# The start of the expert stage: the first chunk's features on another DMA queue, and all bias matrices made at the beginning

## The chip, the cores and the metric

The kernel runs on one core of a Trainium2 chip. The metric is the device time of one execution in microseconds (us); lower is better. Engines: TensorE (PE) does matrix products, VectorE (DVE), ScalarE (ACT) and GpSimd (POOL) do elementwise work, and SyncE (SP) issues most of the DMAs. GpSimd issues DMAs too, on a second queue that is fed by software. Everything is in float32.

## What is computed

Two images of 256 channels and 64x64 positions (4096 tokens each) go through three blocks: a selective-scan block, a bidirectional selective-scan block, and a dense mixture of eight experts. The change concerns the mixture alone, which in the reference is

```
feat = mean over the batch of x                    # x: layer-normed tokens [batch, token, 256]
w    = softmax(feat @ Wr + br)                     # per token, 8 experts; shared by both images
h    = relu(bn(x @ W1[e] + b1)); h = relu(bn(h @ W2[e] + b2))
y    = h @ Wo[e] + bo[e]
out  = t + sum over e of y * w[:, e]
```

## The kernel before

The work is in two stages. The long first stage runs both scan blocks, with DVE and POOL nearly always busy. It also fills TensorE's spare time: as soon as 512 tokens of one image are final, their features are normed and written to DRAM (`nf_dram`), and some of their expert outputs are computed early and written to DRAM (`u_dram`).

The second stage, here called the last stage, does what is left. Work is cut into chunks of 512 tokens, `i` = 0 to 7, for each image `b`. `first[b, i]` is the number of experts that were done early for that chunk. In this build the list of chunks that are not finished, `rest`, is 4, 3, 2, 1, 5, 0. In five of them image 1 has all eight experts left (`first` is 0), and in chunk 5 it has two left (`first` is 6); image 0 is finished everywhere. That makes 42 pairs of a chunk and an expert, taken one after another.

For each pair TensorE runs two layers from PSUM to SBUF through ScalarE (`layer`, matmuls on L1326, evictions on L1330). VectorE then multiplies the result by the token's expert weight (`weigh`, L1337), and three pairs later TensorE runs the third layer and adds into a PSUM tile `y` (`last_layer`, L1350). Before a chunk's first pair in `last_layer`, `y` is opened with a product of the expert weights `wts` and the output biases (L1344). The biases are a matrix `bo_k` of 8 rows by 256, of which the rows below `k = first[b, i]` are zero. `late_bias` makes it: for `k` = 0 a DMA, for another `k` a memset on VectorE (L1305) and then a DMA by SyncE (L1306). It makes each once, at the first call. The kernel before calls it once at the beginning, for chunk 4 (`bo_0`), and otherwise from within `last_layer`, when a chunk is opened. So `bo_6` is made when chunk 5 is opened.

The router's weights come from the sum of both images' features (`both`, for chunk 4 an addition on POOL, L1211), the product with `wr` (`logits`, L1228), a softmax in small steps on VectorE and ScalarE, a transpose (`spread`, L1253), and a trip through DRAM to spread them over partitions (L1257 out, L1259 back). `wr` is scaled on VectorE once (L1379), after its DMA.

Each engine and each queue runs its instructions in the order in which the program emits them. Weights `W1`, `W2`, `Wo` of an expert are loaded by SyncE (`load_w`, L1319) and stay in SBUF. In each round of the loop three matrices are loaded (four in the first), until all are there. Early outputs (`u`, L1274) and residuals (`x`, L1270) are loaded by SyncE too, and added on VectorE (L1275, L1276). The features of chunk 4, for both images, are loaded by POOL's queue (`load_n`, L1182), as are `wr` and `br` (L1377, L1378). In that queue they stand behind the stores of the first stage's last early outputs (L1024).

The beginning of the last stage in the kernel before:

```
load_n(chunks[0])                                   # POOL's queue: chunk 4, both images
wr = ...; br = ...                                  # POOL's queue
nc.vector.tensor_scalar(wr, wr, 1.0 / NB, ...)      # L1379
for name, e in [W1, W2 of expert 0; W1, W2 of 1]:   # SyncE
    load_w(name, e)
late_bias(first[NB - 1, rest[0]])                   # bo_0: SyncE
layer_norm(rest[0]); both(rest[0])                  # no work here; POOL adds
...
for at, (b, i, e) in enumerate(pairs):              # loads, then two layers, ...
```

Of the kernel before, what the change touches and what calls it, by code (L numbers as in the profile page):

```python
# [48 lines left out]
NB, C, L = 2, 256, 4096  # L49
# [33 lines left out]
E = 8  # L83
# [53 lines left out]
def hybrid_kernel(ctx: ExitStack, tc: tile.TileContext, a: dict, out: bass.AP):  # L137
    nc = tc.nc
# [55 lines left out]
    with ExitStack() as st:  # L194
# [790 lines left out]
        def emit_experts(put):  # L985
# [40 lines left out]
            for b, c, e, times in put:  # L1026
                key = {"tag": f"{b}{c}_{e}"}
                early[b, c] = e + 1
                if e == 0:
                    at = max(before.get(0, 0) + 3, min(r[0] for r in ready if r[1:] == (b, c)))  # L1030
                    sl.put(at, "sp", lambda b=b, c=c: load_n(b, c))
                sl.put(times[0], "pe2", lambda b=b, c=c, key=key: key.update(n=n[b, c]))
                for l, (x, dst) in enumerate((("n", "h1"), ("h1", "h2"), ("h2", "u"))):
                    at = before.get(l, times[0] - 6) + 3
                    sl.put(at, "sp", lambda l=l, e=e, key=key: load_w(l, e, key["tag"]))
                    for m in range(KC):
                        slot = before[l] = times[l * KC + m]
                        pe, act = layer(x, dst, l, m, e, key)
                        sl.put(slot, "pe2", pe)
                        sl.put(slot + 1, "act", act)  # L1040

                by = nc.gpsimd if times[-1] + 3 > 2 * nq - 8 else nc.sync
                queue = "pool" if times[-1] + 3 > 2 * nq - 8 else "sp"
                sl.put(times[-1] + 3, queue, lambda b=b, c=c, e=e, key=key, by=by: store(b, c, e, key, by))
# [60 lines left out]
        for g in range(nq):  # L1105
            i, jp, n = quads[g]
# [47 lines left out]
    with ExitStack() as st:  # L1154
# [5 lines left out]
        n, x, y, acc, wts, wb, lt, w_dram = {}, {}, {}, {}, {}, {}, {}, {}  # L1160
        q = T // P
        first = {(b, i): early.get((b, i), 0) for b in range(NB) for i in range(NCH)}
# [3 lines left out]
        rest, whole = [], []  # L1166
# [2 lines left out]

        rest.sort(key=lambda i: (len([b for b in range(NB) if (b, i) not in featured]), sum(first[b, i] for b in range(NB))))  # L1170

        def load_n(i):

            for b in range(NB):
                if first[b, i] == E and i != rest[0]:
                    continue
                n[b, i] = mk.tile([P, KC, T], F32, tag="n", name=f"n_{i}{b}", bufs=4)
                if (b, i) in featured:
                    src = nf_dram[b][:, i, :, :]
                else:  # L1180
                    src = t_dram[b][:, :, i * T : (i + 1) * T]
                nc.gpsimd.dma_start(n[b, i], src)  # L1182

        def summand(name):
            homes.append(homes.pop(0))
# [4 lines left out]
        def layer_norm(i):  # L1190
            for b in range(NB):
                if (b, i) in featured or (b, i) not in n:
                    continue
                v = n[b, i]
                mean = psm.tile([P, T], F32, tag="pm", name=f"mean_m{i}{b}")
                for k in range(KC):
                    nc.tensor.matmul(mean, mean_w, v[:, k, :], start=(k == 0), stop=(k == KC - 1))
                nc.vector.tensor_tensor(v, v, over_channels(mean), ALU.subtract)
                sq = mk.tile([P, KC, T], F32, tag="h0", name=f"sq_{i}{b}", bufs=2)
                nc.scalar.activation(sq, v, AF.Square)  # L1200
                var = psm.tile([P, T], F32, tag="pm", name=f"var_m{i}{b}")
                for k in range(KC):
                    nc.tensor.matmul(var, mean_w, sq[:, k, :], start=(k == 0), stop=(k == KC - 1))
                r = mk.tile([P, T], F32, tag="r", name=f"r_{i}{b}", bufs=1)
                rsqrt(r, var, eps5)
                nc.vector.tensor_tensor(v, v, over_channels(r), ALU.mult)
# [94 lines left out]
        def late_bias(k):  # L1301
            if k not in bo:
                bo[k] = mw.tile([E, C], F32, name=f"bo_{k}")
                if k:
                    nc.vector.memset(bo[k], 0.0)  # L1305
                nc.sync.dma_start(bo[k][k:, :], a["bo"][k:, :])  # L1306
            return bo[k]
# [6 lines left out]
        def load_w(name, e):  # L1314
            if (name, e) in kept:
                we[name, e] = ep.tile([P, KC, C], F32, tag=f"ew{kept.index((name, e))}", name=f"{name}_{e}")
            else:
                we[name, e] = mw.tile([P, KC, C], F32, name=f"{name}_{e}")
            nc.sync.dma_start(we[name, e], a[name][e].rearrange("(k p) n -> p k n", p=P))  # L1319
# [45 lines left out]
        chunks = rest[:1]  # L1365
# [5 lines left out]
        total = sum(item[0] for item in ahead)  # L1371
        todo = [(i, fn) for i in chunks[1:] for fn in routes(i)]

        load_n(chunks[0])
        wr = mw.tile([P, KC, E], F32, name="wr")
        br = mw.tile([P, E], F32, name="br")
        nc.gpsimd.dma_start(wr, a["Wr"].rearrange("(k p) e -> p k e", p=P))  # L1377
# [1 line left out]
        nc.vector.tensor_scalar(wr, wr, 1.0 / NB, None, ALU.mult)  # L1379
        for name, e in [("W1", order[0]), ("W2", order[0]), ("W1", order[1]), ("W2", order[1])]:  # L1380
            load_w(name, e)
        late_bias(first[NB - 1, rest[0]])
        layer_norm(rest[0])
        both(rest[0])
        for i in rest[1:2]:
            load_n(i)
# [192 lines left out]
```

## Time and profile before

| what | value |
|---|---|
| median of 3 runs | 5022.16 us (5012.03 to 5026.47) |
| the profiled execution | 5016.2 us, of which its span 5014.4 us |
| TensorE, share of the span | 85% |
| VectorE / ScalarE / POOL, share of the span | 91% / 72% / 87% |
| last stage's first instruction (SyncE, W1) | 4482.06 us |
| last stage's first matmul | 4501.97 us |
| last matmul | ends 5009.5 us |

The shares are of the whole span, and the first stage makes up nine tenths of it; they say little of the last stage. The profile gives places in us from the start of the span. A row of the timeline has start, busy us, engine, line, operation, out<-in, count, and in brackets how long the engine was idle before it and what ended that. A row of a group has the busy time and mean ns of one, and after a bar the idle time in front of the group. A row of the chain of waits has start, us and what it was spent on. In the table of windows each engine has its busy us and its number of instructions, then come the granted clock of TensorE, the DMA engines' busy share and GB/s.

### The profile page before, as it was taken

The page shows a single profiled execution, that of the slowest core. Times are in us where ns is not written, and L with a number is a line of the kernel's source. Part 1 is how long each engine was busy: PE and PEld are TensorE (multiplying, and loading weights), DVE is VectorE, ACT ScalarE, POOL GpSimd, SP SyncE. Part 2 cuts the span into 40 slices and gives each one's busy share as a digit, 9 for nine tenths or more (in the row PEclk, how much of TensorE's full clock was granted, in tenths as well). Part 3 has the DMA queues.
Part 4 walks back from the last instruction along what each step waited for, and adds up shares of the span by engine and source line. Part 5 has one row for each costly group of instructions (what it writes and reads, how often), then busy time and mean ns, then how long its engine had stood idle before and what let it go on. Part 6 is the DMA issues. An engine that isn't in the chain of part 4 may idle for free. (4 is left out here: it accounts for less than half of the span.)

```text
span 5014.4 us, 47345 instructions
## 1 busy us (share of the span) xinstructions
PE 4249.1 (85%) x14912; PEld 1469.9 (29%) x14912; DVE 4569.4 (91%) x3097; ACT 3617.5 (72%) x7304; POOL 4341.7 (87%) x1426
## 2 busy tenths in 40 slices
PE   5777778778776899989999998889868899889999
PEld 1222222222222233333333233323212333334443
DVE  6998999999999999999999999999999999955664
ACT  5777777777777788877787788888767888752222
POOL 5998999999999999999999999999999999950000
PEclk8778899999887999999999999999989999999999
DMA  5454454444444544456766555554434554445643
GB/s 191 156 188 168 157 166 156 153 145 158 157 160 144 187 173 169 170 174 236 253 231 206 170 178 189 171 190 174 154 135 148 185 190 177 170 153 208 217 157 117
DMA packets 335407, 875.26 MB, mean 175 GB/s; under 512 B 36314, under 2 KB 111860, under 8 KB 293172
## 3 DMA queue, kind: packets, MB, share of 16 engines
q1 hardware_dynamic: 325876, 834.34, 47.8%
q0 software_dynamic: 9280, 37.90, 2.8%
q8 instruction: 118, 1.93, 0.2%
q14 instruction: 133, 1.09, 0.1%
HBM read 673.27 MB, written 198.84 MB: 174 GB/s over the span
## 5 line engine op out<-in xcount | busy, mean ns | idle before, releaser
L742 POOL TENSOR_TENSOR bq<-rxdt,bc 128x2048 f32<-128x2048 f32 x640 | 2893.2, 4542 | 15.4 <-DMA rxdt<-xdtd 7.5
L752 ACT ACTIVATE da<-rdt,w_a 128x512 f32<-128x512 f32 x2560 | 1756.9, 686 | 114.3 <-DVE bq L778 68.2
L778 DVE TENSOR_TENSOR_SCAN da<-da,h_state,bq 128x1024 f32<-128x1024 f32 x664 | 1558.1, 2346 | 56.6 <-ACT da L752 44.2
L803 POOL TENSOR_TENSOR bq<-bq,bc 128x2048 f32<-128x2048 f32 (+1 forms) x280 | 1180.2, 4215 | 22.6
L778 DVE TENSOR_TENSOR_SCAN bq<-da,h_state,bq 128x1024 f32<-128x1024 f32 x456 | 1059.6, 2339 | 20.0 <-ACT da L752 19.7
L811 PE MATMUL y<-bq,stack 128*32 128x512 f32 x5120 | 746.3, 667 | 253.7 <-POOL bq L803 228.3
L787 DVE TENSOR_TENSOR bq<-da,bc 128x1024 f32<-128x1024 f32 x760 | 926.3, 1219 | 15.7
L992 PE MATMUL e<-eh,ew 128*128 128x512 f32 x1376 | 664.8, 617 | 55.1 <-DVE sp L594 13.9
L797 ACT COPY h_state<-da 128x2 f32<-128x2 f32 x759 | 119.2, 157 | 631.6 <-DVE bq L787 628.0
L763 ACT ACTIVATE bq<-h_state,bq,a 128x1 f32<-128x1 f32 x1120 | 429.8, 384 | 2.9 <-POOL bq L742 2.2
L992 PEld LDWEIGHTS e<-eh,ew 128*128 128x128 f32 x1376 | 248.5, 193 | 465.6 <-issue 231.9
L458 PE MATMUL z<-nx,w_in 128*128 128x512 f32 x640 | 324.8, 636 | 62.2 <-DVE q L423 21.2
L811 PEld LDWEIGHTS y<-bq,stack 128*32 128x32 f32 x5120 | 141.0, 116 | 800.0 <-POOL bq L803 343.5
L531 PE MATMUL conv<-xs,w_conv 64*64 64x512 f32 x2560 | 346.9, 617 | 32.1 <-ACT xs L515 29.8
L992 PE MATMUL e<-en,ew 128*128 128x512 f32 x688 | 327.2, 608 | 26.4 <-DVE xr L891 16.5
L1330 ACT ACTIVATE h<-hp,of,sc 128x512 f32<-128x512 f32 x168 | 130.6, 777 | 301.4 <-PE hp L1326 284.2
L458 PE MATMUL xs<-nx,w_in 128*128 128x512 f32 x640 | 316.6, 622 | 34.8 <-DVE sz L624 20.5
L843 PE MATMUL o<-sz,w_out 128*128 128x512 f32 x640 | 295.4, 601 | 0.0
L1005 ACT ACTIVATE eh<-e,of,sc 128x512 f32<-128x512 f32 x344 | 260.2, 769 | 48.4 <-PE e L992 48.2
L598 POOL TENSOR_TENSOR xdt<-sp,xc 128x512 f32<-128x512 f32 x160 | 203.2, 1274 | 50.4 <-DVE sp L594 50.4
L778 DVE TENSOR_TENSOR_SCAN da<-da,bq 128x1024 f32<-128x1024 f32 x96 | 219.4, 2286 | 4.2 <-ACT da L752 2.2
L818 PE MATMUL y<-xc,w_d 128*128 128x512 f32 x320 | 185.0, 662 | 20.3 <-DVE sz L824 20.3
(145 smaller groups left out, 4701.9 us busy)
## 6 DMA issues: line engine op xcount, KB each, us to landing
rxdt<-xdtd SPq DMA_DIRECT2D x160, 1024.0 KB, 6.2
rdt<-dtd SPq DMA_DIRECT2D x160, 1024.0 KB, 6.7
bc<-bcd SPq DMA_DIRECT2D x384, 256.0 KB, 3.2
ew<-in_W SPq DMA_DIRECT2D x172, 256.0 KB, 4.8
u<-u SPq DMA_DIRECT2D x86, 512.0 KB, 5.5
u<-eu SPq DMA_DIRECT2D x82, 512.0 KB, 4.4
dtd<-sp SPq DMA_DIRECT2D x160, 256.0 KB, 3.3
xdtd<-xdt SPq DMA_DIRECT2D x160, 256.0 KB, 3.7
```

The source lines that it names most:

```text
L458: nc.tensor.matmul(ps, job.matrices["in", half][:, k, j * P : (j + 1) * P], rhs, start=(k == 0), stop=(k == KC - 1),)
L531: nc.tensor.matmul(v[r][64 * col : 64 * col + 64, :], job.matrices["conv"][rows, 2 * jp + j, k, :], ck["xs", jp][rows, j, k : k + T] if k ...
L742: nc.gpsimd.tensor_tensor(bq[g], ck["rxdt", j], over_groups(ck["bc", 0, sg]), ALU.mult)
L752: nc.scalar.activation(da[g, h][:, k, :], cks[i]["rdt", j][:, q, :], AF.Exp, scale=steps[i][0].w["a"][:, j, q * SG + sg : q * SG + sg + 1],)
L763: nc.scalar.activation(bq[g][:, q, 0:1], job.h[:, j, sg, q : q + 1], AF.Identity, scale=cks[i]["a0", j][:, h, sg : sg + 1], bias=bq[g][:, ...
L778: nc.vector.tensor_tensor_scan(b if on_pool(g, h) else d, d, b, job.h[:, j, sg, 2 * h : 2 * h + 1] if c else 0.0, ALU.mult, ALU.add,)
L787: nc.vector.tensor_tensor(bq[g][:, two, :], d, cks[i]["bc", 1, sg].rearrange("p (o t) -> p o t", o=1).to_broadcast([P, 2, T]), ALU.mult,)
L803: nc.gpsimd.tensor_tensor(b, b, cks[i]["bc", 1, sg].rearrange("p (o t) -> p o t", o=1).to_broadcast([P, groups, T]), ALU.mult,)
L811: nc.tensor.matmul(y[i, j][q * CG : (q + 1) * CG, :], stack, bq[g][:, q, :], start=False, stop=(sg == SG - 1),)
L843: nc.tensor.matmul(v[m], job.w["out"][:, j, m * P : (m + 1) * P], ck["sz", j], start=False, stop=(j == job.nj - 1),)
L992: nc.tensor.matmul(ps, ew[l][:, k, m * P : (m + 1) * P], key[x][:, k, :], start=(k == 0), stop=(k == KC - 1),)
L1005: nc.scalar.activation(key[dst][:, m, :], key["ps", l, m], AF.Relu, bias=of[:, l, e, m : m + 1], scale=sc[:, l, e, m : m + 1],)
```

## The change

The first chunk's features are loaded by SyncE's queue, in front of the weights, instead of POOL's. And `late_bias` is called at the beginning for every unfinished chunk and image, so that both matrices that this build has, `bo_0` and `bo_6`, are made there; the later calls find them made.

```
-        def load_n(i):
+        def load_n(i, queue=nc.gpsimd):
...
-                nc.gpsimd.dma_start(n[b, i], src)
+                queue.dma_start(n[b, i], src)
...
-        load_n(chunks[0])
+        load_n(chunks[0], nc.sync)
...
         for name, e in [("W1", order[0]), ("W2", order[0]), ("W1", order[1]), ("W2", order[1])]:
             load_w(name, e)
-        late_bias(first[NB - 1, rest[0]])
+        for i in rest:
+            for b in range(NB):
+                if first[b, i] < E:
+                    late_bias(first[b, i])
         layer_norm(rest[0])
```

## The prediction

> **What bounds the kernel now.** I read the table of windows over the last stage first. From 4540 to 4860 us TensorE is busy 314 of 320 us, while VectorE is busy 189 and POOL 16. So after its start this stage is TensorE's, and a pause of TensorE there is a pause of the kernel. Two windows stand out:
>
> ```profile
> 4490.00:4502.00 12.00, 0.03 (x1) 0.06 (x1) 0.00 (x0) 0.00 (x0) 3.31 (x6) 0.61 1.05 347
> 4908.00:4927.00 19.00, 11.62 (x23) 4.23 (x21) 9.12 (x9) 3.11 (x4) 0.00 (x0) 0.80 0.44 157
> ```
>
> In the first, no compute engine but POOL works, and the DMA engines are full (1.05). In the second TensorE works 11.6 of 19 us. The groups of TensorE in this stage give the idle time a name:
>
> ```profile
> L1326 PE MATMUL hp<-n,W 128*128 128x512 f32 x336 | 157.6, 613 | 13.3 <-DMA Wo<-in_Wo 13.3
> L1344 PE MATMUL y<-wts,bo 8*128 8x512 f32 x24 | 13.6, 693 | 7.4 <-DMA bo<-in_bo 7.4
> ```
>
> The name `Wo` in the first row misleads, for the first matmul reads only `n` and `W1`. The timeline of the start shows what was late:
>
> ```profile
> 4482.06 1.98 SPq L1319 DMA_DIRECT2D W<-in_W  x4
> 4490.25 0.53 POOL L1024 DMA_DIRECT2D u<-eu  x1 [7.14 <-ACT eu L1001]
> 4491.18 1.06 POOL L1182 DMA_DIRECT2D n<-nf_dram  x2 [0.40 <-DMA W<-in_W]
> 4492.23 0.71 POOL L1377 DMA_DIRECT2D wr<-in_Wr  x1
> 4501.55 2.33 POOL L1211 TENSOR_TENSOR nm<-n,n 128x1024 f32<-128x1024 f32 x1 [8.05 <-DMA n<-nf_dram]
> 4501.97 5.83 PE L1326 MATMUL hp<-n,W 128*128 128x512 f32 x8 [13.26 <-DMA Wo<-in_Wo]
> 4502.01 1.91 DVE L1379 TENSOR_SCALAR wr<-wr 128x16 f32<-128x16 f32 x1 [37.05 <-DMA x<-t_dram]
> ```
>
> SyncE asks for W1 at 4482.06; POOL asks for the features only at 4491.18, since its queue first holds the store of the last early output, which waits for ScalarE. The addition that reads both features starts at 4501.55, TensorE 0.4 us later. By the trace's semaphore records the first W1 landed at 4485.3 and the two features at 4499.1 and 4501.4. So TensorE waits for features that queue behind a store and then share full DMA engines with some 3 MB of weights. TensorE's first-stage work ends at 4488.7.
>
> The chain of waits shows the second pause:
>
> ```profile
> 4921.53 0.27 DVE bo L1305
> 4921.80 0.02 issue
> 4921.81 1.26 DMA bo<-in_bo
> 4923.07 0.14 issue
> 4923.21 3.75 PE y L1344 x4
> 4926.96 6.64 PE y L1350 x8
> ```
>
> TensorE's layers before it end at 4915.84. The memset of `bo_6` stands in VectorE's order behind five operations on `u`, `x` and `h`, the first of which waited for a `u` to land; SyncE's small DMA waits for the memset, and TensorE for the DMA. After the pause the matmuls are slow as well. The same rows for chunk 1 read
>
> ```profile
> 4817.33 1.91 PE y L1344 x4
> 4819.24 3.63 PE y L1350 x8
> ```
>
> so the pause costs 7.37 us of idling and (3.75 + 6.64) - (1.91 + 3.63) = 4.85 us of slow matmuls, 12.2 us in all.
>
> [...] the pause at 4915 is followed by 4.85 us lost, and the ten records from 4501.97 take 6.69 us where they take 4.29 later, 2.4 us lost. [...] POOL's features took 7.9 and 9.7 us for 512 KB each beside SyncE's loads. [...] The scaling of `wr` is 16 elements a partition and lasts 1.91 us here; it ends at 4503.92, just as POOL's addition does (4501.55 + 2.33).
>
> **The change, step by step.**
>
> *Features on SyncE.* Two issues of about 0.5 us each (the row x4 in 1.98 us) go in front of W1, and each of the four matrices is issued 1.1 us later, W1 at about 4483.2. All that the features wait for in POOL's queue is done by then: the last TensorE projection (4478.1), and the store of the last residual, which SyncE's W1 waits for now too (landed 4481.8). In that ring the features and W1 come to 1.25 MB, behind a 256 KB load of Wo, with a 512 KB store of `u` on the other queue. The kernel before moved 1.5 MB on SyncE's queue with the same store beside it by 4490.97 (Wo of expert 0). So W1 lands near 4490.8, and TensorE starts there instead of 4501.97: 11.2 us. Bounds: 4489, TensorE free and packets of the features faster, gives 13; 4494 gives 8. TensorE then idles 2.1 us instead of 13.3. After the pause of 1.7 us at 4542.4 the next work lost 0.6 us on the transposes (1.01 for 0.44) and 1.1 on the layer (5.41 for 4.29), 1.7 us. Against 2.4 us now that gains 0.7; bounds 0 and 2.4.
>
> *`wr`, `br`.* POOL's two features go from in front of them, so `wr` is issued at 4490.8 and has only the `u` store ahead in its queue: 512 KB took 3.1 us on quiet engines, 6 on full ones. I expect `wr` at 4494.5, bounds 4493 and 4501.7 (as now). POOL's addition runs from about 4492. TensorE needs the scaled `wr` at start + 9 us, about 4500. It is covered; if `wr` came as late as now, TensorE would wait some 4 us here.
>
> *Both biases at the start.* Of the memset (0.27 us) and one 8-row DMA (issue 0.3 to 1 us) nothing is new; they move. But the memset stands on VectorE behind the scaling of `wr`, and SyncE's DMA behind the memset. **SyncE stands still** from about 4486.3 until about 4495.5, and behind it wait Wo of expert 0, W1 and W2 of expert 2 and all later loads, which now go out from 4485.1 on. TensorE needs W1 of expert 2 at the third pair. Now that begins 18.9 us after the first (4520.88 - 4501.97), 18.2 with the warmer start, so at 4509.0. With the memset done at 4495.5, three issues of 0.5 us later W1 goes out at 4497 and lands by 4500.5 (3.2 us) to 4503.5 (6.5). It is hidden with 5.5 to 8.5 us to spare. I cost it at nothing; bound -4.
>
> *What comes late next.* The loads held up (ten matrices, `x`, three `u`, chunk 3's features, some 5 MB at the 0.37 MB per us seen here) end near 4511, the router's trip through DRAM begins near 4510 and must bring chunk 3's sum 2.6 us before it is needed now (landed 4538.10, product at 4540.71). In the next round, with loads beside it, that load took 11.6 us for 8.0. I take 0; bound -3.
>
> *The second pause.* `bo_6` has long landed. `y` has its other inputs, since the `h` of three pairs ago was weighed by 4906; and SyncE's `u` loads no longer stand behind the bias. Gain 12.2; bounds 7.4 (the slow clock stays) and 12.2.
>
> Sum: 11.2 + 0.7 + 0 + 0 + 12.2 = **24.1 us**. Against the profiled execution's own time, 5016.2, that is 4992.1. The median of the runs is 6 us above it, so on the median I forecast 5022.2 - 24.1 = **4998 us**. About 0.3%, 15 us, is what a measurement of this kernel can tell from no change.
>
> **The rivals.**
>
> *The SyncE stall bites.* If `wr` lands as late as now, the memset ends at 4504.2 and W1 of expert 2 lands between 4509 and 4512: TensorE waits up to 4 us at the logits and up to 3 at the third pair, and cools each time by some 2 us. Gain 24 - 7 - 4 = 13 us: 5009. For it: `wr` took 9.5 us. Against it: that was behind 1 MB of features in its queue.
>
> *The features gain little.* If 1.25 MB on SyncE's queue is no quicker, or W1 is now what is late, TensorE starts near 4498 and the front gives 4 us: 16 in all, 5006. For it: DMA engines at 0.92 in 4482 to 4490. Against: the same queue landed as much by 4491. Were the features held by the same store as in POOL's queue (the change not doing what it says), the front gives 0: 5010.
>
> *Slower: the weights starve TensorE.* The place is SyncE's wait for the memset. Each us that the memset ends after about 4503 costs TensorE one. The gain of 24 is gone when it ends near 4527, and the kernel measurably slower from 4542: 5038 us. It would take a `wr` that needs 45 us to land. For it is only the length of the order POOL, VectorE, SyncE; against it are the 9.5 us of now.
>
> **How the numbers follow.** The forecast has 0.70, the stall 0.12, the features that gain little 0.12, slower 0.06. Of the forecast's share, with bounds of 13 to 26 us, 0.66 lies over 15 us; of the second case half, and of the stall 0.05. So faster 0.78, same 0.16, slower 0.06. The range takes the best bound (27 us with the full warm start) and both weaker rivals, with the few us by which medians here differ: 4986 to 5012.
>
> **What would show it.** Right: TensorE's first L1326 near 4491 with some 2 us idle before it; the two features issued by SyncE at 4482; `bo` issued twice before 4500, the second after a gap of some 9 us in SyncE's issues; L1344 with no idle time; last matmul 24 us earlier. Wrong: a wait of L1326 for W at the third pair, of L1228 for `wr` or the sum, or a first matmul after 4495.

## The result, and the profile after

The changed kernel takes 5001.2 us (median of 6 runs, 4996.0 to 5004.4) against 5020.2 us before (6 runs). The ratio is 0.9962 with a 95% interval of 0.9949 to 0.9975: 19 us faster, with an interval of 13 to 26 us. The forecast was 24.1 us faster and 4998 us.

The profiled execution of the changed kernel took 5004.4 us, its span 5002.6. Its last stage began 5.8 us later than in the profile before (first DMA at 4487.82 instead of 4482.06 us), though nothing in the first stage was changed. So times in the last stage are counted here from its first DMA by SyncE.

The timeline of the changed kernel's start, to be read against the one of before:

```profile
4487.82 0.88 SPq L1182 DMA_DIRECT2D n<-nf_dram  x2
...
4488.75 2.58 SPq L1319 DMA_DIRECT2D W<-in_W  x4
...
4491.37 11.10 SPq L1306 DMA_DIRECT2D bo<-in_bo  x2
...
4496.41 3.67 PE L1326 MATMUL hp<-n,W 128*128 128x512 f32 x8 [1.95 <-DMA W<-in_W]
...
4501.94 0.27 DVE L1305 MEMSET bo<- 8x256 f32 x1
4502.11 0.78 ACT L1330 ACTIVATE h<-hp,of,sc 128x512 f32<-128x512 f32 x1 [1.22 <-PE hp L1326]
4502.52 0.40 SPq L1319 DMA_DIRECT2D Wo<-in_Wo  x1
```

SyncE asks for the features first. TensorE starts 8.6 us after that instead of 19.9, and idles 1.95 us instead of 13.26. The row of `bo` covers two DMAs: SyncE issues `bo_0`, stands still for about 10 us, and goes on only when the memset is done. TensorE's groups in the last stage:

```profile
L1326 PE MATMUL hp<-n,W 128*128 128x512 f32 x336 | 158.6, 616 | 1.9 <-DMA W<-in_W 1.9
L1350 PE MATMUL y<-h,Wo 128*128 128x512 f32 x336 | 151.2, 594 | 0.0
L1228 PE MATMUL lt<-wr,nm 128*128 128x8 f32 x128 | 14.9, 251 | 1.0 <-DMA nm<-nf_dram 1.0
L1344 PE MATMUL y<-wts,bo 8*128 8x512 f32 x24 | 11.9, 613 | 0.0
...
L1253 PE MATMUL wt<-ident,w 128*8 128x128 f32 x32 | 6.0, 323 | 8.4 <-DVE w L1247 8.4
```

The two big waits are gone. A small new one is there, on `nm`, the sum of chunk 3's features for the router, and the idle time in front of the transposes (L1253) grew from 7.0 to 8.4 us. The chain of waits where chunk 5 is opened shows the second pause gone and the matmuls fast (granted clock 1.00 from 4913.00 to 4921.40):

```profile
4913.00 2.84 PE hp L1326 x6
4915.84 1.91 PE y L1344 x4
4917.75 3.63 PE y L1350 x8
```

The new wait has its cause some 20 us ahead of it. The timeline:

```profile
4514.29 0.52 POOL L1257 DMA_DIRECT2D w_dram<-wts  x1 [11.89 <-ACT wts L1255]
...
4519.67 0.54 POOL L1259 DMA_DIRECT2D wb<-w_dram  x1 [4.86 <-DMA w_dram<-wts]
...
4528.39 0.90 POOL L1215 DMA_DIRECT2D nm<-nf_dram  x1 [7.66 <-DMA nm<-nf_dram]
...
4533.97 1.92 PE L1228 MATMUL lt<-wr,nm 128*128 128x8 f32 x16 [0.97 <-DMA nm<-nf_dram]
...
4539.03 1.01 PE L1253 MATMUL wt<-ident,w 128*8 128x128 f32 x4 [3.14 <-DVE w L1247]
```

A 16 KB write of the router's weights to DRAM makes POOL wait 4.86 us; in the kernel before it waited 1.5. The table of windows, over the time from the write's issue to its landing, shows the DMA engines full (1.03) with the loads that SyncE had held up:

```profile
4514.29:4519.14 4.85, 4.84 (x12) 2.01 (x11) 0.00 (x0) 2.06 (x3) 0.52 (x1) 1.00 1.03 409
```

In the kernel before they were nearly idle then (0.05). All that follows on POOL's queue is late by the difference: the weights for all partitions (so VectorE's weighing and adding, and after them chunk 3's softmax) and the two loads of chunk 3's sum.

The two profiles have the same matmuls in the same order, so they can be set side by side, each matmul's start counted from the stage's first DMA. So counted TensorE gains 11.3 us at its first matmul and 2.2 more as its first matmuls are faster (granted clock 1.00 over the first ten, where the kernel before had 0.50 from its first matmul to 4506.3), loses 3.3 around chunk 3's router, loses 4.4 net through slow matmuls after later short pauses (4.6 at two of them, with the clock at 0.50 for 6.83 us from 4727.97 and for 3.41 us from 4867.91; 0.2 gained back at a third), and gains 12.2 at the second pause: 18.0 us at the last matmul.

### The profile page after: what moved, and what is told of

It reads as the page before. It is cut to its first block, busy times and chain, and to the rows that moved or that the text cites. A ratio compares the mean times of both kernels' runs of the same rounds, so it can differ in the third digit from the quotient of the medians.

```text
span 5002.6 us, 47346 instructions
## 1 busy us (share of the span) xinstructions
PE 4256.4 (85%) x14912; PEld 1473.8 (29%) x14912; DVE 4568.5 (91%) x3097; ACT 3617.3 (72%) x7304; POOL 4342.2 (87%) x1424
## 5 line engine op out<-in xcount | busy, mean ns | idle before, releaser
L458 PEld LDWEIGHTS z<-nx,w_in 128*128 128x128 f32 x640 | 123.6, 202 | 266.3 <-issue 146.8
```

What stands on the lines that cost most here:

```text
L458: nc.tensor.matmul(ps, job.matrices["in", half][:, k, j * P : (j + 1) * P], rhs, start=(k == 0), stop=(k == KC - 1),)
```

## The experiments

Each kernel was run beside the kernel before on the same chip, whose median was 5020.8 us (26 runs) beside the first four experiments and 5020.6 us (19 runs) beside the others. The row "before" is that of the result above. The write's second number is the busy share of the DMA engines from its issue to its landing. Times in the last stage are again from its first DMA by SyncE.

| kernel | runs, median us | ratio (95% interval) | first L1326, idle before it | write of `w_dram` lands after, DMA share meanwhile | chunk 3: idle before L1228, L1253 | idle before chunk 5's L1344 | last matmul |
|---|---|---|---|---|---|---|---|
| before | 6, 5020.2 | | 19.9, 13.3 | 1.8, 0.05 | 0, 1.74 | 7.37 | 527.4 |
| changed | 6, 5001.2 | 0.9962 (0.9949 to 0.9975) | 8.6, 1.95 | 4.9, 1.03 | 0.97, 3.14 | 0 | 509.4 |
| changed, once more | 1, 4997.3 | | 8.8, 2.2 | 4.9, 1.03 | 1.40, 3.21 | 0 | 505.4 |
| features alone | 21, 5010.0 | 0.9978 (0.9972 to 0.9985) | 9.2, 2.5 | 1.8, 0.09 | 0, 1.74 | 7.48 | 517.4 |
| biases alone | 6, 5003.5 | 0.9968 (0.9956 to 0.9980) | 15.0, 8.3 | 1.8, 0.16 | 0, 1.74 | 0 | 509.2 |
| memset first | 5, 4997.6 | 0.9956 (0.9943 to 0.9968) | 8.7, 2.0 | 1.9, 0.18 | 0, 1.74 | 0 | 502.3 |
| memset first, other order | 5, 4995.8 | 0.9954 (0.9942 to 0.9967) | 7.2, 0.5 | 1.8, 0.06 | 0, 1.74 | 0 | 505.9 |
| SyncE held 7.6 us more | 5, 5002.1 | 0.9964 (0.9951 to 0.9977) | 8.7, 2.1 | 5.0, 1.05 | 2.82, 2.57 | 0 | 512.8 |
| SyncE held 14.8 us more | 15, 5011.0 | 0.9983 (0.9975 to 0.9991) | 8.2, 1.6 | 1.8, 0.07 | 0, 1.74 | 0 | 518.6 |

**The features alone.** The change without its second part:

```
-        for i in rest:
-            for b in range(NB):
-                if first[b, i] < E:
-                    late_bias(first[b, i])
+        late_bias(first[NB - 1, rest[0]])
```

> The features of chunk 4 are loaded by SyncE as in the changed kernel, and bo_6 is made late, as in the kernel before. Theory (front and second pause are separate, and SyncE's wait for the memset is what makes the router's DRAM trip and chunk 3's sum late): counted from the first DMA of the last stage, the first L1326 at 8.6 us with about 2 us idle before it, as in the changed kernel; SyncE issues its loads without a gap, so the trip out on L1257 lands in some 2 us instead of 4.85 and L1228 of chunk 3 does not wait; the second pause is back with 7.4 us idle and some 5 us of slow matmuls. Last matmul 13 us earlier after the stage's start than in the kernel before, minus what the clock takes. Time about 5020 - 12 = 5008 us. Rival (the router's trip is late because TensorE comes to it earlier, whatever SyncE does): L1228 of chunk 3 waits 1 us and its softmax is late here as well, and the gain is about 9 us: 5011.

It gained 11 us (8 to 14). TensorE's waits in its last stage:

```profile
PE y L1344 <- DMA bo<-in_bo: 7.5, 1, 7.5
PE wt L1253 <- DVE w L1247: 7.0, 4, 1.7
PE hp L1326 <- DMA W<-in_W: 2.5, 1, 2.5
PE var_m L1203 <- ACT sq L1200: 2.5, 1, 2.5
PE lt L1228 <- DVE wr L1379: 0.7, 1, 0.7
```

The front is that of the changed kernel, and the second pause is the one of before. TensorE comes to the router's trip 1.5 us later than in the changed kernel and 12 us earlier than in the kernel before, but the write lands in 1.8 us, and neither chunk 3's product nor its softmax is late: each L1253 has its usual 1.7 us. So an early TensorE alone doesn't make the trip late; the long hold below shows it at the very time of the changed kernel. The 0.7 us on L1228 is chunk 4's, which waits for `wr`. Unlike expected, SyncE's issues had a gap, of 3.3 us between W1 and W2 of expert 2; no matmul waited for these. Behind chunk 3's router TensorE is 13.5 us ahead of the kernel before; slow matmuls after later short pauses leave 10.0 at the last matmul. The time, 5010.0 us, lies between the two expectations, so it is the trace that decides.

**The biases alone.** The change without its first part:

```
-        load_n(chunks[0], nc.sync)
+        load_n(chunks[0])
```

> Both bias matrices are made at the start, and the features stay in POOL's queue behind the store. Theory: L1344 of chunk 5 does not wait and the second pause's 12.2 us go. SyncE stands still from some 4 us after its first load until the memset is done; as nothing but four matrices shares the DMA engines with the features then, they land in 4 to 6 us instead of 8 to 10, and the first L1326 comes at about 15 us after the stage's start instead of 19.9: some 5 us more. In all -12.2 - 5 = -17 us: 5003. Rival (the two parts are independent, the front stays as it was): -12.2, 5008. Second rival (SyncE's wait starves TensorE, since wr is later here than in the changed kernel): a wait of L1326 for W at the third pair of some 3 us, and -9 us, 5011.

It gained 16 us (10 to 22), more than the second pause's 12.2. The timeline of its start:

```profile
4486.08 15.42 SPq L1306 DMA_DIRECT2D bo<-in_bo  x2
...
4492.68 1.06 POOL L1182 DMA_DIRECT2D n<-nf_dram  x2 [0.40 <-issue]
...
4499.05 3.52 PE L1326 MATMUL hp<-n,W 128*128 128x512 f32 x4 [8.32 <-DMA br<-in_br]
```

SyncE stands still for 15 us between its two `bo` DMAs. The features, asked for by POOL nearly as late as in the kernel before (8.6 us after the stage's start, for 9.1), land 4.5 and 5.3 us after their issue instead of 7.9 and 9.7, and TensorE starts at 15.0 us instead of 19.9. So SyncE's stop itself gave the front most of 5 us, and the gains of the two parts, 11 and 16, don't add up to the 19 of both: these 5 us of the front are in each of them, and the 3.3 us lost around chunk 3's router come only with both. No pair waited for weights.

**The memset first.** In the changed kernel the scaling of `wr` is emitted behind the bias loop:

```
-        nc.vector.tensor_scalar(wr, wr, 1.0 / NB, None, ALU.mult)
         for name, e in [("W1", order[0]), ("W2", order[0]), ("W1", order[1]), ("W2", order[1])]:
             load_w(name, e)
         for i in rest:
 ...
+        nc.vector.tensor_scalar(wr, wr, 1.0 / NB, None, ALU.mult)
```

> The changed kernel with the scaling of wr emitted after the bias loop, so that the memset of bo_6 does not stand behind it on VectorE and SyncE need not stop. Theory (SyncE's stop of 11 us pushes its loads onto the router's DRAM trip): no gap over 2 us in SyncE's issues, L1257's transfer lands in 2 to 3 us instead of 4.85, no wait of L1228 for chunk 3 (1.0 us in the changed kernel), and the 3.1 us that TensorE lost there are back. First L1326 and second pause as in the changed kernel. About 3 us faster than the changed kernel: 4998. Rival (the stop is hidden and the loss at chunk 3 has another cause): as the changed kernel, 5001. Second rival (the stop gave the first features and W1 quiet DMA engines; without it more loads are in flight): the first L1326 later by 1 to 3 us, and wr later, 5002 to 5004.

Its timeline:

```profile
4486.15 0.27 DVE L1305 MEMSET bo<- 8x256 f32 x1 [17.17 <-DMA t_dram<-xr]
...
4489.53 1.54 SPq L1306 DMA_DIRECT2D bo<-in_bo  x2
...
4515.70 0.54 POOL L1259 DMA_DIRECT2D wb<-w_dram  x1 [1.88 <-PE hp L1326]
...
4531.85 1.85 PE L1228 MATMUL lt<-wr,nm 128*128 128x8 f32 x16
```

The memset stands ahead of the scaling in VectorE's order now, and runs 0.1 us after the stage's start instead of 14.1. The two `bo` DMAs go out one after the other. The write of the router's weights lands in 1.9 us, and chunk 3's product has no wait in front of it. TensorE starts where it did (8.7 us). Set side by side with the second profile of the changed kernel (the last experiment), TensorE gets back 3.4 us at chunk 3; against that chunk 4's logits now wait 0.4 us for `wr`, which lands at 16.2 us instead of 13.3, so that the last matmul comes 3.0 us earlier. The second rival was right about `wr`, then, and wrong about the start. The time is 3.6 us under the changed kernel's, as expected, but the two intervals overlap; the trace carries this verdict, not the time. SyncE still pauses 2.4 us in one place, where no more than 2 was expected: the load of W1 of expert 2 goes out at 4493.88, when the second features have landed (4493.87), the DMA eight places ahead of it in SyncE's queue.

**Another order of the first loads.** On top of that, SyncE loads only what the first pair needs in front:

```
-        load_n(chunks[0], nc.sync)
+        load_n(chunks[0], nc.sync, [NB - 1])
...
+        load_w("W1", order[0])
+        load_w("W2", order[0])
+        load_n(chunks[0], nc.sync, [0])
+        load_w("W1", order[1])
+        load_w("W2", order[1])
```

> As the kernel with the memset first, and SyncE loads only what the first pair needs in front: image 1's features, W1 and W2 of expert 0, then image 0's features (for the router's sum alone), then W1 and W2 of expert 1. Theory (in the changed kernel the landing of W1, last of 1.25 MB, sets TensorE's start): the first L1326 starts when TensorE's first-stage work is done, some 6.7 us after the stage's first DMA instead of 8.6, with under 0.5 us idle before it; the logits do not wait, since image 0's features land by 9 us. About 2 us faster than the kernel with the memset first: 4996. Rival (latency and the store on the other queue set the landing, not the order): start as in the changed kernel, 4998.

TensorE started at 7.2 us, 1.5 us earlier than with the memset first, and its waits there fell to

```profile
PE lt L1228 <- DVE wr L1388: 0.8, 1, 0.8
PE hp L1326 <- DMA W<-in_W: 0.5, 1, 0.5
```

So the order of the first megabyte sets the start, as the theory said, though the start came 0.5 us later than expected. 0.4 us of it was given back at once, since the logits of chunk 4 now wait 0.8 us for `wr`. In this profile slow matmuls followed after that wait and after three of the short pauses, more than in the profile with the memset first; net they took some 4.7 us, and the last matmul came 3.6 us later than there. So the profile does not show a net gain. The time, 4995.8 us, is the lowest median of all kernels here, 24 us under the kernel before (ratio 0.9954); against the kernel with the memset first the difference is inside the intervals.

**SyncE held longer.** Two kernels let SyncE wait on, to see what its stop costs past the point where it is now. Between the memset and the load of `bo_6`:

```
+                    hop = drp.tile([E - k, C], F32, name="hop")
+                    for r in range(3):          # 6 in the second kernel
+                        nc.sync.dma_start(hop, bo[k][k:, :] if r else bo[0][: E - k, :])
+                        nc.sync.dma_start(bo[k][k:, :], hop)
                 nc.sync.dma_start(bo[k][k:, :], a["bo"][k:, :])
```

> The changed kernel, with SyncE held longer: between the memset of bo_6 and its load stand six small DMAs by SyncE, each waiting for the one before (out to DRAM and back, into rows that the true load then writes over). At about 2.1 us each SyncE resumes some 12.6 us later than in the changed kernel, where W1 of expert 2 landed 5.5 us before the third pair needed it. Theory (that slack is all that hides SyncE's stop; past it each us costs one): L1326 of the third pair waits about 7 us for W and runs cold for some 2 us after; chunk 3's sum is then no longer late, which gives 3 us back. About 6 us slower than the changed kernel: 5007. Rival (loads catch up, so a longer stop stays hidden): 5001. Second rival (all later loads are late too, x, u and the other weights, and TensorE waits at several pairs): over 12 us, 5013 or more.

> The same with twelve such DMAs: SyncE resumes some 25 us later than in the changed kernel. Theory: the wait of L1326 at the third pair grows by the whole added time, to about 20 us, with the same 2 us of cold matmuls and the same 3 us back: about 19 us slower than the changed kernel, 5020, which is the time before the change. Rival (the stop is mostly hidden): under 5010. Second rival (more waits come at later pairs): 5030 or more.

The small DMAs took 1.1 to 1.5 us each, save one of 2.5, not 2.1, and the first didn't wait for the memset. So SyncE was held 7.6 and 14.8 us more than in the changed kernel (the load of `bo_6` at 22.0 and 29.2 us instead of 14.4), and the expected sizes have to be read for these doses. From the timeline of the short hold:

```profile
4508.73 3.70 PE L1330 MATMUL hp<-n,W 128*128 128x512 f32 x8 [0.29 <-DMA W<-in_W]
...
4526.94 3.70 PE L1354 MATMUL y<-h,Wo 128*128 128x512 f32 x8 [1.75 <-DVE h L1341]
...
4533.46 1.70 PE L1228 MATMUL lt<-wr,nm 128*128 128x8 f32 x14 [2.82 <-DMA nm<-nf_dram]
```

The third pair waits only 0.3 us for its weights. The loss is in the router's trip: the write takes 5.0 us, the weights for all partitions 10.6 us instead of 7.0, and TensorE waits for the weighing and for chunk 3's sum. Set side by side, this costs 3.3 us more than in the changed kernel's first profile. In the times, 5002.1 against 5001.2, nothing of it can be told. From the long hold:

```profile
4520.03 5.49 PE L1330 MATMUL hp<-n,W 128*128 128x512 f32 x6 [13.94 <-DMA W<-in_W]
```

Here the third pair waits 13.9 us for W1 of expert 2, and goes on with slow matmuls (six in 5.49 us, where the short hold took 3.70 for eight), which costs 3.0 more. With 5.5 us of slack the added 14.8 would explain 9.3 of the wait; the rest is that W1 landed about 9.0 us after its issue instead of 4.5, now itself beside the router's loads on POOL's queue. The router's trip runs ahead of SyncE's loads:

```profile
4507.22:4509.00 1.78, 0.00 (x0) 0.00 (x0) 0.00 (x0) 0.00 (x0) 0.52 (x1) 0.95 0.07 12
```

The write lands in 1.8 us, and chunk 3 is not late. This is the closest test of what delays the write. It is issued 26.1 us after the stage's start here, 26.5 and 26.7 in the two profiles of the changed kernel and 26.6 in the short hold; it lands in 1.8 us where SyncE's loads are not yet out (DMA share 0.07), and in 4.9 to 5.0 where they are (1.03 to 1.05). How the DMA engines divide their time between the two queues is not shown. After chunk 3's router TensorE is 13.7 us behind the first profile of the changed kernel. The time is 10 us above the changed kernel's and still 8.5 us under the kernel before. The theory's place was right for the long hold and wrong for the short one, where the loads' collision with the router's trip came first; and it left out that the two collide the other way round too.

**The changed kernel once more.**

> The changed kernel once more, with an empty line in front, for a second profile of the same program (line numbers are one higher). Theory (two slow stretches after equal pauses, 2.9 us at chunk 1's transposes and 1.7 us at the last chunk's norm, belong to that execution and not to the change): first matmul 8.6 us after the stage's first DMA, chunk 3's sum late by about 1 us and its softmax by 1.4 us as before, but no slow stretch, or other ones, after the pauses of 1.74 and 2.46 us. Rival (they come with the change's timing): both are there again at the same places.

The chain of waits at chunk 1's transposes, in the first profile of the changed kernel and in the second:

```profile
4728.96 1.01 PE wt L1253 x4
4729.97 6.76 PE hp L1326 x10
```

```profile
4726.19 0.60 PE wt L1254 x4
4726.78 4.29 PE hp L1327 x10
```

Both follow a pause of 1.74 us. In the first profile the transposes and the matmuls after them are slow and 2.9 us are lost; in the second they are not, and the 1.7 us at the last chunk's norm are back too. The table of windows, from 1 us before the transposes on, gives the granted clock, half in the first profile and full in the second:

```profile
4727.96:4734.79 6.83, 5.83 (x10) 2.58 (x11) 2.92 (x5) 1.54 (x3) 2.08 (x4) 0.50 0.37 112
```

```profile
4725.19:4732.02 6.83, 5.82 (x16) 2.59 (x17) 2.92 (x5) 2.32 (x4) 2.13 (x4) 1.00 0.41 119
```

Chunk 3's sum and softmax are late in both. So the 3.3 us lost around chunk 3's router belong to the change, and the 4.6 us to that execution. In the second profile the last matmul comes 22.0 us earlier than in the kernel before, after 18.0 in the first.

## Why the prediction was right, and where it was off

- **What bounds the stage** held: TensorE, and two pauses of it. Each part taken alone removed its own pause, and the features alone left the other as it was; the biases alone shortened it too, from 13.3 to 8.3 us.
- **Features on SyncE.** Forecast 11.2 us earlier, measured 11.3 and 11.1. The landing of W1, last of 1.25 MB, sets the start: 1.95 us idle was left, 2.1 in the forecast, and the other order cut it to 0.5.
- **The warm start** was sized too small: 0.7 us against 2.2. After its pause of 1.95 us TensorE ran the first ten records (matmuls in the trace) in 4.53 us, where 6.69 were needed before. I had taken the pause of 1.74 us before chunk 3's transposes as the model, where the granted clock fell to 0.50 for 3.41 us; at chunk 1's transposes in the same profile, after an equal pause, it stayed at 1.00.
- **`wr`** landed 12.9 us after the stage's start, where I had 12.4, and TensorE did not wait for it. In part that was luck: `wr` was issued 1.7 us later than forecast, and landed in 2.5 us instead of 3.7. In the three kernels that load the features by SyncE and don't stop it, `wr` took some 5.6 us and landed at 15.0 to 16.7, and the logits waited 0.4 to 0.8 us. SyncE's stop cleared the way for it, which I had not counted.
- **SyncE's stop.** It came, and the memset ended 14.4 us after the start (forecast 13.4). It was late because the scaling of `wr` began at 13.2 beside POOL's addition and took 0.96 us; the same step of before, at 1.91 us, stands in the prediction's own lines. W1 of expert 2 landed 5.5 us before it was needed, 4.7 in the second profile. The weights were hidden, as forecast, and with 14.8 us more they were not.
- **What comes late next: the step that failed.** I named the place, the router's trip and chunk 3's sum, gave it a bound of 3 us, and took 0. It cost 3.3 us in both profiles. I had counted the 2.6 us of slack and looked for contention in the load of chunk 3's sum; the delay was in the 16 KB write ahead of it, 4.9 us instead of 1.8, and everything on POOL's queue inherits it. With the memset first, the stop and the delay go together.
- **The second pause.** Forecast 12.2, measured 12.2 in both profiles, the slow matmuls included.
- **The slow clock.** Around the second pause of the kernel before the granted clock was half for 13.65 us, 9.76 of them at work:

```profile
4919.32:4932.97 13.65, 9.76 (x11) 3.69 (x12) 8.41 (x8) 0.00 (x0) 0.00 (x0) 0.50 0.31 117
```

The sum took the cost of both slow stretches from the trace, 4.85 and 2.4 us.

In sum 11.1 + 2.2 - 3.3 + 12.2 = 22.2 us, against the 22.0 of the second profile; slow matmuls after short pauses took 4.4 more in the first. Two terms were off in opposite directions, 1.5 us of the warm start and the 3.3 lost at the router's trip were both left out, so the sum came nearer than its parts. The measured 19 us has an interval of 13 to 26, so that the 5 us between it and the forecast can't be split further from the times. The gains of the two weaker rivals, 13 and 16 us, lie in this interval too; it is the traces that exclude them. Of the rivals, the stop that bites at the weights needs some 7 us more hold than there is, and the features that gain little is out, with the first matmul at 8.6 and 8.8 us and not near 16. The slower one lies beyond what was tried: 14.8 us more hold left the kernel 8.5 us faster than before. One slip: the shares that the prediction adds up for a faster kernel, 0.66, half of 0.12 and 0.05, give 0.77, not 0.78.

## What to carry to other kernels

When an edit puts a wait into a load queue, don't ask only which matrix behind it is needed first. The loads held up came out later as one block here, and what paid was the chain of DMAs that then met them: a 16 KB write that a broadcast and two loads wait for. An operation whose inputs are ready, as this memset, belongs ahead of one that waits for a DMA on the same engine; moving it gave 3.4 us back in the traces and cost 0.4 at the logits. And two edits that share a queue have to be tried one by one: alone they gave 11 and 16 us, together 19. What the change gave is not what its best form gives: with the memset first the traces show some 3 us more, which the times can't confirm.

## What the runs showed of the hardware

- The same pause doesn't always cost the same. After 1.74 us of idling and the four transposes that end it, the next ten records took 4.29 us in one execution of the changed kernel and 6.76 in another. It differs within one execution too: in the kernel before, after equal pauses of 1.74 us, the transposes and the next ten records took 0.60 and 4.29 us at chunk 1, with the granted clock at 1.00, and 1.01 and 5.41 us at chunk 3, where the clock was 0.50 for 3.41 us, from 0.3 us ahead of the transposes. Up to the last matmul of the last stage, the stretches at 0.50 lasted 13.65, 3.41, 3.41, 3.41 and 13.65 us in the profile of the kernel before and 6.83, 3.41, 6.83, 3.41 and 3.41 us in the first profile of the changed kernel: 3.41 us, twice or four times that. What begins and ends them is not shown.
- The first 16 KB write of the router's weights, from SBUF to DRAM on POOL's queue, landed in 1.8 to 1.9 us with the DMA engines 5% to 18% busy, and in 4.9 to 5.0 us with the engines full.
- SyncE had at most eight DMAs under way where the landings are recorded. In the profiles of the kernel before and of the changed kernel, from 30 us before the stage's start to 60 us after it, none of 56 issues came ahead of the landing of the DMA eight places before it, and 6 came within 0.06 us after it. Whether the program or the hardware sets this is not shown.
- The first stage, the same in all kernels, ended between 4481.1 and 4487.8 us in nine profiles. From single profiles, a difference of a few us in this kernel can be read only from inside the stage that was changed.
- The scaling of `wr`, 16 elements a partition, took 0.17 us with POOL's addition over (memset first). Beside it, it took 1.91 us in the kernel before, 0.96 and 0.84 in the changed kernel's two profiles, 2.04 with the biases alone and 0.87 in the short hold, and in all five it ended within 0.05 us after the addition. What holds it up is not shown.
